# Projected pairs in an attention kernel: where the two sums of rows are issued, and in which order the products follow each other

## The chip, the cores and the metric

One NeuronCore of a Trainium2 chip runs the whole program. The metric is the device time of one execution in microseconds (us). The kernel before took 934.48 us (median of 3 runs, 934.42 to 935.12).

## The reference

Inputs are `x` of 16 batches x 100 rows x 640, and a context of 16 x 722 x 384 whose last 4 rows are "tokens". All is float32. Cut to what matters:

```python
enc, ca = ctx[:, :718], ctx[:, 718:]
hs      = mha(x @ Wq, enc @ Wk, enc @ Wv)           # 8 heads of 80, softmax over 718 keys
ca_q1   = einsum('btc,th->bch', ca, Wq_ca)[:, indices]
ca_hs1  = mha(ca_q1, x, x)
ca_hs2  = mha(ca_hs1 @ Wq, ca @ Wk_ca, ca @ Wv_ca)  # softmax over the 4 tokens
out     = (hs + ca_hs2) @ Wout + b_out + x
```

The change concerns the last line, the projection of the 1600 rows of `hs + ca_hs2` by the 640 x 640 matrix `Wout`, and the place of the weighted sum over the four tokens' values (in `ca_hs2`) on GpSimd's queue.

## The kernel before, in words

One loop runs over the 16 batches (L1198). The order of the work in it is written out by hand: the scheduler is told to keep it (L1197), so each engine takes its instructions in the order of the source. In a batch, TensorE makes the scores of three groups of keys (`scores`, L612), then, interleaved by hand, the blocks of this batch's values and of the next batch's keys (`vv.go`, `kk.go`, `both`; L432 and L463), then the last chunk of keys (`last_keys`, L557), the projection of earlier rows where enough rows are ready, the queries of the next two batches (L533, every second batch), and at the end the product of probabilities and values (L1417). Beside that VectorE takes maxima and subtracts them (L1232, L1220), ScalarE copies from PSUM and takes exponentials, and GpSimd does elementwise work on SBUF: scores of the tokens (L761, L768), the bias added to `x` (L895), probabilities of the tokens (L841), the weighted sum of the tokens' values (`values2`, L855 and L862), sums of context chunks (L498) and masked products (L709).

**The projection of a pair.** The 1600 rows are cut into chunks of 128, and ten of them are taken as five pairs. A pair is projected in the batch after the one that ended its rows, so in batches 3, 6, 8, 11 and 13 (`PAIRS`, L39). Of the 640 inner columns the first four chunks of 128 are multiplied by a scheme of seven block products in place of eight; the fifth chunk (`last(k)`) is added by plain products. The blocks are two chunks deep, so a block product is two matmuls of 128 x 128 by 128 x 320. Each float32 matmul is two records in the trace, hence 36 records for the 18 matmuls of a pair. `one` and `two` are the transposed rows of the pair's chunks, and `w(i, k)` the blocks of `Wout`.

The scheme needs sums of rows and of weights, all on GpSimd:

- `sums` (L986): `sum1` = the two blocks of `two` added, then the first block of `two` := `sum1` minus the first block of `one` (both L994). It is issued after `values2` (L1326 to L1328).
- in `project_pair` (L996): the second block of `one` is reduced by the first of `two` (L1030), the first block of `two` is replaced by the second minus itself (L1033), and the sum of weights `wout2[:, 0]` is reduced by `w(0, 0)` (L1034).

The products go into four PSUM banks, `b1`, `b2` of their own and `b3`, `b4`, the halves of one two-bank tile. `read(bank, j, k)` (L1022) has VectorE add a bank to the output rows of chunk `j`, columns half `k` (L1024, 128 x 320). `b1` is a running sum: it is read after each of its first three products and accumulated on, so each further product in `b1` waits until VectorE has read the bank. Between two uses of `b1` stand products in other banks.

The order before, in matmuls: `b1` 2, `b2` 3, `b1` 2 (needs the second L994), `b4` 3, `b1` 2 (with `sum1`), `b3` 2 (needs L1033 and L1034), `b1` 3 (needs L1030), `b3` 1.

**Queues.** SyncE issues most loads in order: in `values2` the third and fourth value rows `vb` (L810, each waits until GpSimd has used the buffer it goes into), then the next `xT` (some batches), `ca`, three pieces of `enc` (L218), `mb` (L700), two of `rest` (L231), and the output rows (L1048). GpSimd's own queue issues the first two `vb` of the next batch (L810) between `sums` and L1030.

Of the kernel before, what the change touches and what calls it, by code (L numbers as in the profile page):

```python
# [125 lines left out]
def kernel(  # L126
# [40 lines left out]
    def psumk(name):  # L167
        return psk.tile([P, 512], F32, tag="psk", name=name)
# [88 lines left out]
    wout2 = const.tile([P, 2, 2, H // 2], F32, name="wout2")  # L257
# [618 lines left out]
    class Last:  # L876
# [119 lines left out]
        def project_pair(self):  # L996

            r = PAIRS[self.b]
            one, two = hsTs[r], hsTs[r + 1]
            w = lambda i, k: wout_sb[  # L1000
                :, 2 * i : 2 * i + 2, k * (H // 2) : (k + 1) * (H // 2)
            ]
            last = lambda k: wout_sb[:, 4:, k * (H // 2) : (k + 1) * (H // 2)]
            both = pair(f"o_ps_{r}")
            b1, b2 = psumk(f"o_ps1_{r}"), psumk(f"o_ps2_{r}")
            b3, b4 = both[:, 0], both[:, 1]
            xn = self.xn
            less, more = ALU.subtract, ALU.add

            def product(to, terms, first):  # L1010
                steps = [(t[:, c], f[:, c]) for t, f in terms for c in range(t.shape[1])]
                for i, (t, f) in enumerate(steps):
                    nc.tensor.matmul(  # L1013
                        to[:, : H // 2],
                        t,
                        f,
                        start=first and i == 0,
                        stop=i == len(steps) - 1,
                        skip_group_check=True,
                    )  # L1020

            def read(bank, j, k):  # L1022
                part = xn[r + j][:, k * (H // 2) : (k + 1) * (H // 2)]
                nc.vector.tensor_tensor(part, bank[:, : H // 2], part, ALU.add)  # L1024

            product(b1, [(one[:, :2], w(0, 0))], True)
            read(b1, 0, 0)
            product(b2, [(one[:, 2:4], w(1, 0)), (one[:, 4:], last(0))], True)
            read(b2, 0, 0)
            nc.gpsimd.tensor_tensor(one[:, 2:4], one[:, 2:4], two[:, :2], less)  # L1030
            product(b1, [(two[:, :2], wout2[:, 0])], False)
            read(b1, 1, 0)
            nc.gpsimd.tensor_tensor(two[:, :2], two[:, 2:4], two[:, :2], less)  # L1033
            nc.gpsimd.tensor_tensor(wout2[:, 0], wout2[:, 0], w(0, 0), less)  # L1034
            product(b4, [(two[:, 2:4], wout2[:, 1]), (two[:, 4:], last(0))], True)
            read(b4, 1, 0)
            product(b1, [(sum1, w(0, 1))], False)
            read(b1, 1, 1)
            product(b3, [(two[:, :2], wout2[:, 0])], True)
            read(b3, 1, 0)  # L1040
            product(b1, [(one[:, 2:4], w(1, 1)), (one[:, 4:], last(1))], False)
            read(b1, 0, 1)
            product(b3, [(two[:, 4:], last(1))], False)
            read(b3, 1, 1)
            rows = out.rearrange("b s n -> (b s) n")
            for j in range(2):
                lo, n = OC[r + j]
                nc.sync.dma_start(out=rows[lo : lo + n], in_=xn[r + j])  # L1048
            xn.clear()
# [139 lines left out]
    last, enc_next, second_next = None, load_rest(1, load_enc(1)), Second(1, xT)  # L1189
# [8 lines left out]
    for b in range(B):  # L1198
        p = b // 2
        e_in, now = enc, second  # L1200
# [57 lines left out]
        if b == 0:  # L1258
            second.scores1()
            m_next = load_m(b + 2)  # L1260
            kk.go(3)
            top.go(3)
            first_values(3, e_in, (act, act), get=bank)
            top.go(1)
            kk.go(2)
            now.scores2()
            now.exponentials2()
            first_values(0, e_in, (act, act), (0,), bank)
            top.go()
            kk.go(3)  # L1270
            first_values(0, e_in, (act, act), (1,), bank)
            now.softmax3()
            kk.go(2)
            subtract(0)
            exponential(0)
            kk.go(2)
            subtract(1)
            kk.go(3)
            exponential(1)
            second_next, enc_next = loads()  # L1280
            less = subtract(2)
            exponential(2)
            last_keys(b + 1, enc)
            enc_next = load_rest(b + 2, enc_next)
            keys(m_next)
            now.values2(less)
            enc_sums(enc_next)
            second.softmax1(4)
        elif b + 1 < B:
            vv = Values(b, e_in)  # L1290

            def both(n):
                vv.go(n)
                kk.go(n)

            forms = [wout_sb[:, 2 * i : 2 * i + 2, k * (H // 2) : (k + 1) * (H // 2)]
                     for i in range(2) for k in range(2)]
            if b == 2:
                for o, left, right in (
                    (forms[1], forms[1], forms[0]),  # L1300
                    (wout2[:, 0], forms[3], forms[1]),
                    (wout2[:, 1], forms[2], wout2[:, 0]),
                ):
                    nc.gpsimd.tensor_tensor(o, left, right, ALU.subtract)
            elif last.b - 1 in PAIRS:
                nc.gpsimd.tensor_tensor(wout2[:, 0], wout2[:, 0], forms[0], ALU.add)
            second.scores1(seen, range(T - 1))
            top.go(3)
            both(3)
            now.scores2(nc.gpsimd)  # L1310
            second.scores1(None, range(T - 1, T))
            if b == 1:
                now.load()
            last.load()
            top.go(1)
            if b > 1:
                last.place()
            now.exponentials2()
            both(2)
            both(2)  # L1320
            top.go()
            both(1)
            now.softmax3()
            if b == 1:
                nc.gpsimd.tensor_tensor(last.hs[:S], last.hs[:S], last.hs2, ALU.add)
            now.values2()  # L1326
            if last.b in PAIRS:
                last.sums()  # L1328
            vv.go(2)
            kk.go(1)  # L1330
            subtract(0)
            exponential(0)
            vv.go(1)
            subtract(1)
            vv.go(1)
            kk.go(2)
            exponential(1)
            vv.go(1)
            kk.go(2)
            both(1)  # L1340
            both(1)
            if b == 1:
                for f in list(wv_there):
                    nc.scalar.copy(wv_sb[:, W_AT[f]], wv_there.pop(f))
            second.load()
            if b == 1:
                nc.gpsimd.dma_start(out=bias, in_=bout[0].partition_broadcast(P))
            second_next, enc_next = loads()
            if b + 2 < B:
                m_next = load_m(b + 2)  # L1350
            subtract(2)
            exponential(2)
            last_keys(b + 1, enc)
            if b + 2 < B:
                enc_next = load_rest(b + 2, enc_next)
            if b == 1:
                last.transpose()
            if last.b in PAIRS:
                second.softmax1(3)
                last.project_pair()  # L1360
                if last.b == max(PAIRS):
                    nc.sync.dma_start(
                        out=forms[1],
                        in_=wout[: 2 * P, H // 2 :].rearrange("(c p) n -> p c n", p=P),
                    )
            second.softmax1()
        else:
            room = enc_tile("spare").rearrange("p f k -> p (f k)")
            spare.extend(room[:, i * H : (i + 1) * H] for i in range(2))
            last.transpose()  # L1370
            vv = Values(b, e_in)
            last.load()
            mine.load()
            top.go(3)
            vv.go(3)
            last.project_few(len(OC) - 2)
            now.scores2(nc.gpsimd)
            now.exponentials2()
            top.go(1)
            vv.go(2)  # L1380
            top.go()
            vv.go(3)
            now.softmax3()
            now.values2()
            vv.go(2)
            subtract(0)
            exponential(0)
            vv.go(5)
            for i in (1, 2):
                subtract(i)  # L1390
                exponential(i)
            last.project()
# [49 lines left out]
        last = mine  # L1442
# [55 lines left out]
```

## Time and profile before

| what | us or share |
|---|---|
| median of 3 runs | 934.48 (934.42 to 935.12) |
| the profiled execution's own time | 933.03 |
| its span, first to last instruction | 931.3 |
| TensorE busy (matmul records) | 924.1, 99% |
| VectorE, ScalarE, GpSimd busy | 690.6 (74%), 433.8 (47%), 680.8 (73%) |
| granted TensorE clock | 0.999 |
| matmuls of the pairs (L1013) | 180 records of 0.432 us each, five stages |
| read of a bank (L1024) | 40 of 0.49 us |
| sums of rows (L994), in each pair | 0.72 and 0.73 or 0.74 us |
| L1030, L1033, L1034, in each pair | 0.74, 0.72, 1.53 us |
| one product and one sum of `values2` (L855, L862), undisturbed | 1.27 and 1.54 us |

The times of single instructions come from the timeline (start, length, engine, line, what is written from what, and in brackets how long the engine was idle before and who released it). PE rows are matmuls, PEld rows their weight loads, DVE is VectorE, ACT ScalarE, POOL GpSimd, and SP SyncE. Matmuls are pipelined: a record is 0.432 us long, and in an undisturbed run the next starts 0.269 us after it. So a stall is read from the distance of starts, not from the idle time in brackets.

### The profile page before, as it was taken

How to read it: one execution, taken by the hardware profiler on the slowest of the kernel's cores; microseconds unless marked ns; L12 is line 12 of the kernel's file. 1: busy time of each engine (PE TensorE's matmuls, PEld its weight loads, DVE VectorE, ACT ScalarE, POOL GpSimd, SP SyncE). 2: the span in 40 equal slices, each digit the busy share in tenths (PEclk: the TensorE clock that was granted, in tenths of full speed). 3: DMA queues.
4: the chain of work that ended last, by engine and by line, in shares of the span. 5: the costliest groups of instructions: out<-in, count | busy, mean ns of one | idle time of the engine just before them, and what ended most of it. 6: DMA issues, size and time to landing. Idle time of an engine off the chain costs nothing.

```text
span 931.3 us, 25889 instructions
## 1 busy us (share of the span) xinstructions
PE 924.1 (99%) x11130; PEld 786.7 (84%) x11130; DVE 690.6 (74%) x1080; ACT 433.8 (47%) x836; POOL 680.8 (73%) x646
## 2 busy tenths in 40 slices
PE   9999999999999999999999999999999999999998
PEld 6998989797797979888798788988879888798966
DVE  3859894989639896795967869579873898738884
ACT  2234543737336363652726436264641737417341
POOL 5757999788937878496874968658895588946723
PEclk9999999999999999999999999999999999999999
DMA  8822022040300304031030400204030050310201
GB/s 260 269 80 77 25 65 77 11 145 2 104 30 20 108 12 121 2 103 53 27 105 3 123 33 30 75 2 154 2 103 30 2 153 2 103 44 2 81 18 42
DMA packets 49673, 62.82 MB, mean 67 GB/s; under 512 B 14072, under 2 KB 38200, under 8 KB 49560
## 3 DMA queue, kind: packets, MB, share of 16 engines
q1 hardware_dynamic: 45512, 51.49, 18.0%
q0 software_dynamic: 3024, 8.53, 3.1%
q8 instruction: 87, 1.43, 0.6%
q10 hardware_dynamic: 1024, 1.15, 0.4%
q14 instruction: 26, 0.21, 0.1%
HBM read 55.59 MB, written 5.57 MB: 66 GB/s over the span
## 4 chain that ended last, share of the span: by engine, by line
PE 89%; POOL 7%; DVE 1%; DMA 1%; issue 1%; ACT 0%; POOLq 0%; DVEq 0%
PE s_ps L612 12%; PE a_ps L1417 12%; PE v_psA L432 9%; PE v_psB L432 8%; PE q_ps L533 7%; PE kT_ps L557 7%; PE k_psA L463 7%; PE k_psB L463 6%; PE o_ps L1013 4%; PE v_psC L432 3%; PE k_psC L463 2%; PE y_ps L736 2%; PE v_psD L432 2%; PE v_ps L373 2%; PE v_psE L432 2%; POOL e L761 1%
## 5 line engine op out<-in xcount | busy, mean ns | idle before, releaser
L761 POOL TENSOR_TENSOR e<-ca,g 100x800 f32<-100x800 f32 x64 | 99.5, 1564 | 127.0 <-DVE most L1232 113.1
L498 POOL TENSOR_TENSOR enc<-enc 128x240 f32<-128x240 f32 x135 | 105.9, 793 | 19.6 <-DMA enc<-in_enct 12.6
L1220 DVE TENSOR_TENSOR st<-st,over 120x1600 f32<-120x1600 f32 x48 | 115.5, 2407 | 0.0
L1417 PEld LDWEIGHTS a_ps<-vs,st 120*36 120x36 f32 (+3 forms) x3072 | 109.3, 125 | 5.3 <-issue 5.2
L1417 PE MATMUL a_ps<-vs,st 120*36 120x81 f32 (+3 forms) x3072 | 112.3, 233 | 0.2 <-issue 0.2
L432 PE MATMUL v_psA<-wv_sb,enc 128*120 128x320 f32 x352 | 109.8, 434 | 0.0
L862 POOL TENSOR_TENSOR hs<-hs,hs 100x640 f32<-100x640 f32 x48 | 103.7, 2160 | 3.8
L855 POOL TENSOR_TENSOR hs<-vb,p 100x640 f32<-100x640 f32 x64 | 91.7, 1444 | 8.9 <-issue 4.7
L612 PE MATMUL s_ps<-qp,kT 32*120 32x100 f32 x3072 | 97.8, 263 | 0.0
L612 PEld LDWEIGHTS s_ps<-qp,kT 32*120 32x120 f32 x3072 | 95.0, 179 | 1.7 <-issue 0.2
L629 ACT COPY st<-s_ps 120x800 f32<-120x800 f32 x64 | 49.7, 829 | 98.7 <-PE s_ps L612 98.7
L768 POOL TENSOR_TENSOR e<-e,e 100x800 f32<-100x800 f32 x48 | 92.2, 1920 | 3.8
L432 PE MATMUL v_psB<-wv_sb,enc 128*120 128x320 f32 x296 | 91.8, 433 | 0.0
L1228 ACT ACTIVATE st<-st 120x1600 f32<-120x1600 f32 x48 | 73.9, 1539 | 31.1 <-DVE st L1220 31.0
L463 PE MATMUL k_psA<-enc,wk_sb 128*128 128x240 f32 x360 | 87.7, 366 | 0.0
L1232 DVE TENSOR_TENSOR most<-most,st 120x800 f32<-120x800 f32 x64 | 68.2, 1065 | 22.4 <-ACT st L623 21.3
L463 PEld LDWEIGHTS k_psA<-enc,wk_sb 128*128 128x128 f32 x360 | 68.2, 190 | 16.8 <-DVE kT L403 0.2
L432 PEld LDWEIGHTS v_psA<-wv_sb,enc 128*120 128x120 f32 x352 | 63.2, 183 | 22.6 <-DVE vs L403 0.5
L463 PE MATMUL k_psB<-enc,wk_sb 128*128 128x240 f32 x300 | 73.1, 366 | 0.3 <-DVE sm L838 0.3
L432 PEld LDWEIGHTS v_psB<-wv_sb,enc 128*120 128x120 f32 x296 | 54.1, 183 | 21.9 <-DVE vs L403 0.4
L928 ACT COPY hsT<-turned_hs 32x160 f32<-32x160 f32 (+7 forms) x244 | 67.7, 278 | 3.0
L533 PE MATMUL q_ps<-xT,wq_sb 128*128 128x200 f32 x400 | 69.1, 333 | 0.0
(168 smaller groups left out, 1800.1 us busy)
## 6 DMA issues: line engine op xcount, KB each, us to landing
vb<-va_d POOLq DMA_DIRECT2D x32, 250.0 KB, 3.6
vb<-va_d SPq DMA_DIRECT2D x32, 250.0 KB
enc<-in_enct SPq DMA_DIRECT2D x30, 240.0 KB
enc<-in_enct SPq DMA_DIRECT2D x15, 360.0 KB
xT<-in_xt SPq DMA_DIRECT2D x8, 500.0 KB
rest<-in_enct SPq DMA_DIRECT2D x31, 120.0 KB
xn<-in_x SPq DMA_DIRECT2D x11, 320.0 KB
out<-xn SPq DMA_DIRECT2D x11, 320.0 KB
```

The costliest lines, as they stand in the source:

```text
L432: nc.tensor.matmul(at[0][j][:KN, : H // 2], a_form(self.enc, f)[:, j * KN : (j + 1) * KN], wv_there.get(f, wv_sb[:, W_AT[f]]), start=first ...
L463: nc.tensor.matmul(at[:, i * KT : (i + 1) * KT], wk_sb[:, W_AT[f], i], a_form(self.enc, f), start=(first and i == 0), stop=last, skip_grou ...
L498: nc.gpsimd.tensor_tensor(out, left, right, op)
L533: nc.tensor.matmul(q_ps[:, : 2 * S].rearrange("p (j s) -> p j s", j=2), wq_sb[:, c, n * P : (n + 1) * P], xT[:, :, c, :], start=(c == 0), ...
L612: nc.tensor.matmul(s_ps[r][:n, 256 * a + lo : 256 * a + hi], kT[rows, c, u, j * KN : (j + 1) * KN], rhs, start=(a == 0 and c == 0), stop=( ...
L761: first = nc.gpsimd.tensor_tensor(to, self.ca[:, t, :].unsqueeze(1).to_broadcast([S, NH, S]), g[:, :, t].unsqueeze(2).to_broadcast([S, NH, ...
L768: nc.gpsimd.tensor_tensor(e, e, to, ALU.add)
L855: first = nc.gpsimd.tensor_tensor(to, self.vb[t][:S].rearrange("p (h d) -> p h d", h=NH), p2[:, :, t].unsqueeze(2).to_broadcast([S, NH, D] ...
L862: nc.gpsimd.tensor_tensor(sums, sums, to, ALU.add)
L1220: return nc.vector.tensor_tensor(st[i], st[i], top.over[:KN].unsqueeze(1).to_broadcast([KN, 2, ROWS]), ALU.subtract,)
L1228: nc.scalar.activation(st[i], st[i], AF.Exp, scale=SCALE)
L1417: nc.tensor.matmul(a_v[lo:hi, h % 4], st[i // 2][: KEYS[i], i % 2, h * S + lo : h * S + hi], block(i, h // 4)[: KEYS[i], h % 4], start=(i ...
```

## The change

Two edits. In `project_pair` the order of the products is altered, the product of the fifth chunk with the second half of the columns moves from `b3` to a second use of `b2` (with a read of its own), and the product that needs the reduced sum of weights comes last and is then read twice. In the loop, `sums` is issued ahead of `values2`.

```diff
             product(b1, [(two[:, :2], wout2[:, 0])], False)
             read(b1, 1, 0)
             nc.gpsimd.tensor_tensor(two[:, :2], two[:, 2:4], two[:, :2], less)
             nc.gpsimd.tensor_tensor(wout2[:, 0], wout2[:, 0], w(0, 0), less)
-            product(b4, [(two[:, 2:4], wout2[:, 1]), (two[:, 4:], last(0))], True)
-            read(b4, 1, 0)
+            product(b4, [(two[:, 2:4], wout2[:, 1])], True)
             product(b1, [(sum1, w(0, 1))], False)
             read(b1, 1, 1)
+            product(b4, [(two[:, 4:], last(0))], False)
+            read(b4, 1, 0)
+            product(b2, [(two[:, 4:], last(1))], True)
+            read(b2, 1, 1)
+            product(b1, [(one[:, 2:4], w(1, 1)), (one[:, 4:], last(1))], False)
+            read(b1, 0, 1)
             product(b3, [(two[:, :2], wout2[:, 0])], True)
             read(b3, 1, 0)
-            product(b1, [(one[:, 2:4], w(1, 1)), (one[:, 4:], last(1))], False)
-            read(b1, 0, 1)
-            product(b3, [(two[:, 4:], last(1))], False)
             read(b3, 1, 1)
...
             now.softmax3()
...
-            now.values2()
             if last.b in PAIRS:
                 last.sums()
+            now.values2()
```

The order after, in matmuls: `b1` 2, `b2` 3, `b1` 2, `b4` 2, `b1` 2 (with `sum1`), `b4` 1, `b2` 1, `b1` 3, `b3` 2. It is 18 matmuls as before, nine reads in place of eight, and the same five operations on GpSimd, of which the two L994 stand ahead of the seven operations of `values2`.

## The prediction

> **What bounds the kernel now.** First the page's busy line and its chain of the work that ended last:
>
> ```profile
> PE 924.1 (99%) x11130; PEld 786.7 (84%) x11130; DVE 690.6 (74%) x1080; ACT 433.8 (47%) x836; POOL 680.8 (73%) x646
> PE 89%; POOL 7%; DVE 1%; DMA 1%; issue 1%; ACT 0%; POOLq 0%; DVEq 0%
> ```
>
> TensorE sets the time: the chain is 89% its own work, and only where another engine holds it up can a reordering gain. POOL's 7% is the one other part worth a look. The view of the line of the pairs' matmuls (L1013) says who holds them up:
>
> ```profile
> its engine sat idle before it (us, times) until:
>   POOL wout L1034: 2.6, 5
>   POOL hsT L994: 2.2, 4
> ```
>
> All by POOL: the second sum of rows (L994), which the second product in b1 needs, and the reduced sum of weights (L1034), which the product in b3 needs. These are idle times of the loads and matmuls added up; what TensorE lost is read from starts. The matmuls of the first pair (batch 3), then POOL beside them:
>
> ```profile
> 244.36 2.85 PE L1013 MATMUL o_ps<-wout_sb,hsT 128*128 128x320 f32 x10
> 247.59 2.42 PE L1013 MATMUL o_ps<-wout,hsT 128*128 128x320 f32 x8 [0.37 <-POOL hsT L994]
> 249.85 0.70 PE L1013 MATMUL o_ps<-wout_sb,hsT 128*128 128x320 f32 x2
> 250.38 1.24 PE L1013 MATMUL o_ps<-wout_sb,sum 128*128 128x320 f32 x4
> 251.68 1.34 PE L1013 MATMUL o_ps<-wout,hsT 128*128 128x320 f32 x4
> 252.86 2.32 PE L1013 MATMUL o_ps<-wout_sb,hsT 128*128 128x320 f32 x8
> 255.01 3.21 PE L533 MATMUL q_ps<-xT,wq_sb 128*128 128x200 f32 x18
> ```
>
> ```profile
> 244.50 1.54 POOL L862 TENSOR_TENSOR hs<-hs,hs 100x640 f32<-100x640 f32 x1
> 246.00 0.72 POOL L994 TENSOR_TENSOR sum<-hsT 128x256 f32<-128x256 f32 x1
> 246.80 0.74 POOL L994 TENSOR_TENSOR hsT<-sum,hsT 128x256 f32<-128x256 f32 x1
> 247.48 1.10 POOL L810 DMA_DIRECT2D vb<-va_d  x2
> 248.59 0.74 POOL L1030 TENSOR_TENSOR hsT<-hsT,hsT 128x256 f32<-128x256 f32 x1
> 249.40 0.72 POOL L1033 TENSOR_TENSOR hsT<-hsT 128x256 f32<-128x256 f32 x1
> 250.09 1.53 POOL L1034 TENSOR_TENSOR wout<-wout,wout_sb 128x640 f32<-128x640 f32 x1
> ```
>
> The last eight records run freely: 2.15 us, 0.269 each. Ten take 2.69, so the row at 247.59 should have begun at 247.05; L994 ended at 247.54. POOL goes from the last step of values2 (L862) through all seven rows almost without a gap: it is simply behind.
>
> **What can be gained.** A free stage of 36 records is 9.68. The five stages, from the first record to the first of the next work, last 10.65, 10.00, 9.99, 10.41 and 10.05 (pairs at 244, 415, 529, 691 and 807): 2.70 over it in all. By the place of the loss:
>
> - Before the second b1 product, and in its row (the second record starts 0.1 late after a stall): 0.54 + 0.11 at 244, 0 at 415 and 529, 0.30 + 0.11 at 691, 0.01 + 0.03 at 807. Sum 1.10.
> - Before b3 and in its row, each from the starts of sum's row, b3's row and the next, less 1.08 for four records: 0.32, 0.21, 0.20, 0.30, 0.32. Sum 1.35.
> - The other 0.2 lies at the step from the last record to L1417 after the pairs at 415 and 529 (0.1 each) and stays.
>
> **Part 1, sums ahead of values2.** It adds no work. POOL has its operands there: the wait of L841 for ScalarE, just ahead, covers the copies that fill the rows (the last ended at 226.4; the sums would start at 234.3). So the second sum is there over 10 us before TensorE asks, and the 1.10 goes. What is late next at that place is VectorE's first read of b1: at 244 it ends at 246.19, and the load it would release is due at 246.78. Values2 ends 1.5 later, where the sums ended before, so L810, L1030, L1033 and L1034 keep their times. Values2's result is added by VectorE only after the product with the probabilities, some 20 us on. SyncE's vb loads wait for values2, and ca (or xT and ca) stand behind them: 1.5 later each, with 1.0 to 1.5 us from the end of that later queue to enc's own release by TensorE (at 244: ca ended at 237.55, plus 1.5 is 239.05; enc was issued at 240.10). So the loads cost nothing; without that cover enc would come some tenths later, and its first reader, L498, stands behind L1034.
>
> **Part 2, the order of the products.** 18 matmuls before and after. b3 moves from the 25th record to the 33rd. Its load is due at start + 31 x 0.269: 252.70 at 244, against L1034's end of 251.62 plus 0.05 for the release (at 415: end 422.16, load at 422.21). Slack 1.03; at the others 1.77, 1.77, 1.27 and 1.62. So the 1.35 goes too. b1's last product needs L1030, which ended 1.7 us before its load would be due.
>
> The price: b1's further products have two matmuls (four records, 1.08 us) as cover where the sum had three. No row shows a four-record cover without a stall by POOL in it, so I bound it. VectorE at the pair at 415, behind its own work:
>
> ```profile
> 416.56 0.64 DVE L676 TENSOR_REDUCE mx<-side 32x25 f32<-32x100 f32 x2
> 417.23 0.49 DVE L1024 TENSOR_TENSOR xn<-o_ps,xn 128x320 f32<-128x320 f32 x1
> 418.53 0.49 DVE L1024 TENSOR_TENSOR xn<-o_ps,xn 128x320 f32<-128x320 f32 x1 [0.82 <-PE o_ps L1013]
> 419.67 0.49 DVE L1024 TENSOR_TENSOR xn<-o_ps,xn 128x320 f32<-128x320 f32 x1 [0.64 <-PE o_ps L1013]
> ```
>
> The last one is the read that sum1's product waits for. Its matmul's last record started at 419.14 and the read ended 1.02 later; with 0.05 for the release that is 1.07, and the load is due after 1.08. Even a late load costs little: at 807 the load that waited for L994 stood idle 0.27 and TensorE lost 0.04; at 691 idle 0.64 lost 0.41. About 0.23 is free. So I take 0. The upper end: 0.2 at each of ten such places, 2.0. The lower end is 0, since a wait gives nothing back.
>
> The ninth read is 0.49 of VectorE in each pair, and now two reads follow the last product where one did; the last ends some 0.3 later than now. Behind it stand L694 and L778 (ends at 428.5 at the pair at 415), for an exponential that TensorE needs after L1417 and the next scores, 14 us on. Hidden; without the cover 0.5 a pair. The first use of b2's bank by the queries is now behind that bank's second read, which ends some 1.8 us before it is wanted.
>
> **One rule against the change.** The same subtraction on VectorE (L1220, 48 times) takes 1.77 to 3.10 us, and POOL's L855 takes 1.27 alone and 2.74 beside one that starts at 410.88. The Trainium skill, SBUF — State Buffer, section "Who interferes with whom", says that a VectorE operation with two SBUF inputs and a GpSimd operation that reads SBUF shut each other out, and the first to start keeps the port. By that rule other POOL operations would meet the subtractions, and values2 would end at another time than 1.5 later; one hold more by it would make the sum 1.75.
>
> By the rows each of a pair's three subtractions costs POOL about 1.5, whatever it meets, since POOL has work throughout. One hold more (1.5 against a slack of 1.03 or 1.27) would leave 0.5 and 0.2 of stall at 244 and 691; the others absorb it. I keep the 2.45 and this 0.7 for the range.
>
> **Sum.** 1.10 + 1.35 = 2.45. The profiled execution's 933.03 would become 930.58. The median of the runs is 1.45 above that execution, with nothing to say where; I take the same 2.45 off: 934.48 - 2.45 = 932.0. A change under 0.2% (1.9 us) is about what measurement can't tell from none.
>
> **The rivals.**
>
> - *The reads set the pace* (the cover of two matmuls falls short at ten places). For: slack of 0.01 by the rows. Against: 0.23 free. At 0.1 a place, 1.0 is given back: 933.0.
> - *POOL's end slips* by a hold: 0.7 given back, 932.7. For: the subtractions shift against POOL's queue. Against: the same three holds in every pair.
> - *The time is waited for elsewhere*: TensorE comes to L1417 earlier and waits for the exponentials: 934.5. Against: the third subtraction ended at 413.8 and its exponential takes 1.54, with L1417 due at 425.6.
> - *Slower: VectorE comes late to the first read of b1.* At 415, 529 and 807 that read follows L676 at once, so it moves with the third subtraction, which may have to wait for a POOL operation. Up to 0.5 it is free (0.29 of slack at 415 and the 0.23), and late by x it costs about 3 times x - 0.5, so from x = 1.3 it eats the gain. Late by 2.0, it costs 4.5 there, and at 244 and 691, where the read now starts 0.7 and 0.9 after L676 and is done 0.5 before the load, 0.6 and 0.3: 937.4. Against: the subtraction there took 2.95 already, and none of 48 took over 3.10.
>
> **How the numbers follow.** Forecast 0.60, the reads 0.18, POOL 0.09, elsewhere 0.08, slower 0.05. Range: up to 934.0 (the reads' upper end, 2.0 given back, is 934.0); down to 931.0, should the runs that are 1.45 longer than the profiled one have lost part of it, say 1.0, at these same waits. It leaves out the last two cases. Faster by over 0.2% (below 932.6): the forecast and part of the POOL case, 0.63. Slower: 0.05. Within: 0.32.
>
> **What would show it.** Right: L1013 idle for POOL near 0; five stages of 9.7 to 9.8; L994 some 10 us ahead of the stage, L1034 at the same distance from the stage's start, and b3's row without idle time. The reads: rows with sum or the last b1 product start over 1.08 after the fourth record before, released by DVE L1024. POOL: L1034 ends over 8.3 after the stage's start. Elsewhere: L1417 or L533 waiting. What makes me wrong: a wait of the new order I priced at 0.

## The result, and the profile after

The changed kernel took 930.79 us (median of 6 runs, 929.97 to 931.6) where the kernel before took 934.68 in the same measurement (6 runs, 934.1 to 935.12): ratio 0.9959, 95% interval 0.9946 to 0.9972. That is 3.9 us faster by the medians (2.6 to 5.0 by the interval) where 2.45 was forecast, and 0.2 us below the range. The profiled execution took 931.33, span 929.5.

The page's busy line and its chain, as shown of before:

```profile
PE 922.4 (99%) x11130; PEld 787.6 (85%) x11130; DVE 693.2 (75%) x1085; ACT 433.9 (47%) x836; POOL 678.2 (73%) x646
PE 97%; DVE 2%; DMA 0%; issue 0%; ACT 0%; POOL 0%; ACTq 0%; DVEq 0%
```

POOL's 7% of the chain is gone, and VectorE has the five reads more. In the view of line L1013 the list of what its engine waited for is empty: there is no row between its heading and "who waited for it". The matmuls of the first pair, then POOL:

```profile
244.40 2.86 PE L1013 MATMUL o_ps<-wout_sb,hsT 128*128 128x320 f32 x10
247.09 2.32 PE L1013 MATMUL o_ps<-wout,hsT 128*128 128x320 f32 x8
249.25 1.24 PE L1013 MATMUL o_ps<-wout_sb,sum 128*128 128x320 f32 x4
250.32 2.85 PE L1013 MATMUL o_ps<-wout_sb,hsT 128*128 128x320 f32 x10
253.02 1.24 PE L1013 MATMUL o_ps<-wout,hsT 128*128 128x320 f32 x4
254.09 2.19 PE L533 MATMUL q_ps<-xT,wq_sb 128*128 128x200 f32 x12
```

```profile
231.16 1.82 POOL L841 TENSOR_TENSOR p<-e,sm 100x32 f32<-100x32 f32 x1
232.95 0.73 POOL L994 TENSOR_TENSOR sum<-hsT 128x256 f32<-128x256 f32 x1
233.75 2.25 POOL L994 TENSOR_TENSOR hsT<-sum,hsT 128x256 f32<-128x256 f32 x1
...
245.96 1.54 POOL L862 TENSOR_TENSOR hs<-hs,hs 100x640 f32<-100x640 f32 x1
247.44 1.10 POOL L810 DMA_DIRECT2D vb<-va_d  x2
248.55 0.74 POOL L1030 TENSOR_TENSOR hsT<-hsT,hsT 128x256 f32<-128x256 f32 x1
249.36 0.73 POOL L1033 TENSOR_TENSOR hsT<-hsT 128x256 f32<-128x256 f32 x1
250.05 1.54 POOL L1034 TENSOR_TENSOR wout<-wout,wout_sb 128x640 f32<-128x640 f32 x1
```

VectorE's reads of the pair at 415, which stood behind its own work in the kernel before too:

```profile
414.86 0.66 DVE L676 TENSOR_REDUCE mx<-side 32x25 f32<-32x100 f32 x2
416.40 0.49 DVE L1024 TENSOR_TENSOR xn<-o_ps,xn 128x320 f32<-128x320 f32 x1 [0.89 <-POOL hs L855]
...
421.19 1.57 DVE L1024 TENSOR_TENSOR xn<-o_ps,xn 128x320 f32<-128x320 f32 x3 [1.60 <-PE o_ps L1013]
423.88 0.49 DVE L1024 TENSOR_TENSOR xn<-o_ps,xn 128x320 f32<-128x320 f32 x1 [1.12 <-PE o_ps L1013]
424.96 0.89 DVE L1024 TENSOR_TENSOR xn<-o_ps,xn 128x320 f32<-128x320 f32 x2 [0.59 <-PE o_ps L1013]
```

VectorE is now early: it sits idle ahead of the first read, where in the kernel before it went straight from L676 to that read. Three later reads come in a row, and the last two follow the last product; all the later ones are released by TensorE. (The view names POOL for the first, but it starts 0.52 after the start of its product's last record, as reads that TensorE released do.) TensorE waits for none of them: in the matmuls of the first pair, every start is the one before plus 0.269 a record. The five stages last 9.69, 9.78, 9.78, 9.69 and 9.69: 48.64 in all where the first profile of before has 51.09. The second L994 ends over 8 us ahead of each stage, some 11 ahead of the product that needs it. L1034 ends 7.18 after the first stage's start where it ended 7.26 after it. So each step of the mechanism stands as forecast, and against the first profile the stages lost exactly the 2.45. What does not fit is the total: by the runs it is 3.9, by these two profiled executions 933.03 - 931.33 = 1.7.

### The profile page after: what moved, and what is told of

Same layout as the page of the kernel before. It is cut to its first block, busy times and chain, and to the rows that moved or that the text cites. A ratio compares the mean times of both kernels' runs of the same rounds, so it can differ in the third digit from the quotient of the medians.

```text
span 929.5 us, 25894 instructions
## 1 busy us (share of the span) xinstructions
PE 922.4 (99%) x11130; PEld 787.6 (85%) x11130; DVE 693.2 (75%) x1085; ACT 433.9 (47%) x836; POOL 678.2 (73%) x646
## 4 chain that ended last, share of the span: by engine, by line
PE 97%; DVE 2%; DMA 0%; issue 0%; ACT 0%; POOL 0%; ACTq 0%; DVEq 0%
PE s_ps L612 12%; PE a_ps L1419 12%; PE v_psA L432 11%; PE v_psB L432 9%; PE kT_ps L557 8%; PE k_psA L463 7%; PE q_ps L533 7%; PE k_psB L463 6%; PE o_ps L1013 5%; PE v_psC L432 3%; PE k_psC L463 3%; PE v_psD L432 2%; PE v_psE L432 2%; PE y_ps L736 2%; PE v_ps L373 1%; PE k_psE L463 1%
## 5 line engine op out<-in xcount | busy, mean ns | idle before, releaser
L761 POOL TENSOR_TENSOR e<-ca,g 100x800 f32<-100x800 f32 x64 | 99.4, 1564 | 126.8 <-DVE most L1234 99.7
L498 POOL TENSOR_TENSOR enc<-enc 128x240 f32<-128x240 f32 x135 | 106.7, 800 | 19.7 <-DMA enc<-in_enct 12.7
L432 PE MATMUL v_psA<-wv_sb,enc 128*120 128x320 f32 x352 | 109.8, 434 | 0.0
L862 POOL TENSOR_TENSOR hs<-hs,hs 100x640 f32<-100x640 f32 x48 | 100.5, 2095 | 3.8
L855 POOL TENSOR_TENSOR hs<-vb,p 100x640 f32<-100x640 f32 x64 | 89.6, 1411 | 9.5 <-issue 4.7
L432 PE MATMUL v_psB<-wv_sb,enc 128*120 128x320 f32 x296 | 91.8, 433 | 0.0
L432 PEld LDWEIGHTS v_psA<-wv_sb,enc 128*120 128x120 f32 x352 | 63.2, 183 | 22.6 <-DVE vs L403 0.5
L432 PEld LDWEIGHTS v_psB<-wv_sb,enc 128*120 128x120 f32 x296 | 54.1, 183 | 21.9 <-DVE vs L403 0.4
```

Source lines behind the costliest of these rows:

```text
L432: nc.tensor.matmul(at[0][j][:KN, : H // 2], a_form(self.enc, f)[:, j * KN : (j + 1) * KN], wv_there.get(f, wv_sb[:, W_AT[f]]), start=first ...
L498: nc.gpsimd.tensor_tensor(out, left, right, op)
L761: first = nc.gpsimd.tensor_tensor(to, self.ca[:, t, :].unsqueeze(1).to_broadcast([S, NH, S]), g[:, :, t].unsqueeze(2).to_broadcast([S, NH, ...
L855: first = nc.gpsimd.tensor_tensor(to, self.vb[t][:S].rearrange("p (h d) -> p h d", h=NH), p2[:, :, t].unsqueeze(2).to_broadcast([S, NH, D] ...
L862: nc.gpsimd.tensor_tensor(sums, sums, to, ALU.add)
```

## The theories

- *A*: the waits for POOL cost more in a usual execution of before than in the one the forecast was worked from; the change takes all of them.
- *B*: the waits are the same in every execution. The profiled one was short for other reasons, and the change gains something the stages do not show.

The table has every profiled execution. "Stages" are the five stretches from the first record of a pair to the first of the next work; the two losses are read from the starts around the second product in b1 (L994) and the product in b3 (L1034); "rest" is time less stages.

| execution | time | stages | lost at L994 | lost at L1034 | rest |
|---|---|---|---|---|---|
| before, the one shown | 933.03 | 51.09 | 1.07 | 1.38 | 881.94 |
| before, second | 934.79 | 52.08 | 2.08 | 1.37 | 882.71 |
| before, third | 934.31 | 52.00 | 1.98 | 1.39 | 882.31 |
| after | 931.33 | 48.64 | 0 | 0 | 882.69 |
| after, second | 930.37 | 48.64 | 0 | 0 | 881.73 |
| sums ahead alone | 934.04 | 51.76 | 0 | 3.12 | 882.28 |
| order alone | 934.76 | 51.51 | 2.88 | 0 | 883.25 |
| order alone, second | 935.11 | 51.80 | 3.16 | 0 | 883.31 |
| order alone, third | 933.92 | 50.80 | 2.17 | 0 | 883.12 |
| before, one POOL operation more | 937.62 | 54.78 | 1.98 | 4.17 | 882.84 |
| after, one POOL operation more | 930.86 | 48.64 | 0 | 0 | 882.22 |
| after, cover of one matmul | 933.85 | 50.51 | 0 | 1.88 (reads) | 883.34 |
| before without the pairs' bias | 931.16 | 48.64 | 0 | 0 | 882.52 |
| after, b3 read between | 936.64 | 54.76 | 0 | 1.88 + 4.25 (reads) | 881.88 |
| before, POOL's start let go | 931.44 | 49.43 | 0.13 | 0.66 | 882.01 |

In the two rows with "(reads)" the loss is VectorE's reads at other places.

## The experiments

**The kernel before, twice more** (no edit).

> The kernel before, unchanged, for a second profiled execution: the one the forecast was made from took 933.03, the runs 934.1 to 935.12. Theory A (what the profiled execution showed too little of is the very waits for POOL in the five pairs; POOL came later in the runs): the five stages exceed 9.68 by some 4 us in all, not 2.70, in an execution of about 934.5, and L994 and L1034 end later against the stage's start. Theory B (the waits in the pairs are the same in every execution, the 1.45 us lies in other places, such as issue stalls or the loads at the start): the stages exceed 9.68 by 2.5 to 2.9 again and the extra time is found elsewhere along the chain.

> A third profiled execution of the kernel before, to tell a property of the kernel from chance. Theory A: again some 4 us over 9.68 in the five stages. Theory B: 2.5 to 2.9 again, the rest elsewhere and at places that differ between the executions.

934.79 and 934.31. Of the second execution, the view of line L1013, and the matmuls of the pair in batch 11:

```profile
  POOL hsT L994: 4.1, 6
  POOL wout L1034: 2.6, 5
```

```profile
693.21 2.85 PE L1013 MATMUL o_ps<-wout_sb,hsT 128*128 128x320 f32 x10
696.79 2.42 PE L1013 MATMUL o_ps<-wout,hsT 128*128 128x320 f32 x8 [0.73 <-POOL hsT L994]
```

The idle time for L1034 is the 2.6 of the first profile; that for L994 is 4.1 in place of 2.2. The second row starts 3.58 after the first where 2.69 is free: 0.90 lost, with 0.10 more in the row, against 0.40 in the first profile. The stages exceed five times 9.68 by 3.7 and 3.6. That is A in kind, a little under its 4; B's 2.5 to 2.9 is excluded.

**Each part alone.** The edits are the two halves of the diff: `sums` ahead of `values2` with the old order of products, and the new order with `sums` behind.

> Part 1 alone: the sums of rows ahead of values2, the products in the old order. It leaves the wait for L1034. By the prediction's terms the wait for L994 (1.10) goes: 933.6 against 934.7. Theory A, with 3.9 gained in all shared like the 2.45: about 1.7 gained, 932.9. Theory B, where the terms are right and the rest is gained by something else: 1.1 and a part of 1.4 more that the stages do not show. In the profile: no idle time for L994, the row with b3 still late by 0.2 to 0.5 or more, since POOL is as late as before and TensorE comes earlier.

> Part 2 alone: the new order of products, the sums behind values2. It leaves the wait for L994. By the prediction's terms the wait for L1034 (1.35) goes: 933.3 against 934.7. Theory A: about 2.1 gained, 932.6. Theory B: 1.35 and a part of 1.4 more that the stages do not show. In the profile: the wait for L994 as before at the pairs of batches 3 and 11, none at b3.

Sums ahead alone: 933.81 (ratio 0.9991, 0.9983 to 1.0). Order alone: 932.55 (ratio 0.9985, 0.9976 to 0.9994); seven of its twelve runs lie at 931.8 to 932.8, the others at 933.1 to 935.7. The sums fall short of the 932.9 that I expected by A and are hardly clear of no gain. The order has the expected 932.6 as its median, but by the ratio, which goes by the means, it gained 1.4 in place of 2.1. The first pair with the sums ahead says why they gain so little:

```profile
247.02 2.32 PE L1013 MATMUL o_ps<-wout,hsT 128*128 128x320 f32 x8
...
249.71 1.24 PE L1013 MATMUL o_ps<-wout_sb,sum 128*128 128x320 f32 x4
251.47 1.34 PE L1013 MATMUL o_ps<-wout,hsT 128*128 128x320 f32 x4 [0.51 <-POOL wout L1034]
```

The row for L994 is on time. The b3 row comes 1.76 after sum's where 1.08 is free: 0.68, and 0.10 in the row. TensorE arrives earlier, POOL does not, and the wait for L1034 takes over: 3.12 in all in place of 1.4. The two waits stand in series behind one late engine. The wait at L994 costs nothing more once the one at L1034 follows, so moving the sums gains little by itself. The new order alone takes the wait at L1034 away in each execution and leaves the one at L994. So my 1.10 for the sums was not what that part is worth alone; only both together move what TensorE needs from POOL out of the way.

**Order alone, twice more**, for its two groups of runs (no further edit).

> Part 2 alone once more, since its runs fell into two groups, near 932.2 and near 934.7, and the profiled one was of the upper group with 2.9 us lost at L994. If the groups differ by how late POOL comes, an execution of the lower group shows 0.5 or less lost there; if by something else, 2.9 again.

> Part 2 alone for a third execution, with the same two outcomes to tell apart: 0.5 or less lost at L994 in an execution near 932.2, or 2.9 again whatever the time.

935.11 with 3.16 lost at L994, 933.92 with 2.17. Time and loss go together over the three executions; none fell into the lower group, so what that group lost was not seen.

The loss at L994 is larger here than in the three executions of before (1.07, 2.08, 1.98), but the new order did not bring it about inside the stage: it is larger in the first pair already, ahead of which nothing of the new order has run (0.87, 1.06 and 1.10, in before 0.64, 0.41 and 0.45). There POOL's chain of the batch (L761) started 28.33 to 28.41 ahead of the stage, in before 28.74 to 28.84. A late start goes with a large loss, as the last experiment takes up; why it was late in all three is open.

**One POOL operation more**, the same edit on before and on the changed kernel, ahead of the first product:

```diff
+            scratch = product_tile(f"scratch_{r}")[:, : 4 * P // 2].rearrange("p (c s) -> p c s", c=2)
+            nc.gpsimd.tensor_tensor(scratch, two[:, 2:4], two[:, 2:4], more)
```

> The kernel before with one more operation of about 0.72 us on POOL at the start of each projection, ahead of L1030, onto a scratch tile that nothing reads. If POOL is what TensorE waits for in every pair (theory A), each of the five waits for L1034 grows by 0.7 to 0.8: 3.5 to 4.0 slower than before, 938.3. If the end is set by something else and POOL's waits take up slack (theory B): less than 2.

> The changed kernel with the same operation at the same place. By the slack that the new order leaves at the product in b3 (1.0 to 1.8 us by the prediction, and 0.2 that a late load has free): no change, 930.8. If the slack is not there, up to 4 slower than the changed kernel, 934.8.

Before: 937.29 (ratio 1.0031, 1.0019 to 1.0043), 2.7 slower. The operation took 0.62 and set the rest back by 0.57, less than the 0.72 I took. The five waits for L1034 grew by 0.55 or so each, in all from 1.38 to 4.17: POOL's delay is passed on whole. On the changed kernel: 931.09 (0.9963, 0.9949 to 0.9977), no loss. POOL of its first pair, whose b3 row began at 252.77:

```profile
247.98 0.63 POOL L1027 TENSOR_TENSOR scratch<-hsT 128x256 f32<-128x256 f32 x1
...
250.04 1.54 POOL L1036 TENSOR_TENSOR wout<-wout,wout_sb 128x640 f32<-128x640 f32 x1
```

The sum of weights ends at 251.58, 1.2 before the row starts, and 0.9 before its load is due. The slack is real.

**POOL's lateness taken away without the change.** In the kernel before, the bias added to the ten paired chunks (L895) is left out, 3.1 us of POOL's work ahead of the sums in each pair; order and place of the sums stay, and the output of those chunks lacks the bias.

```diff
-                    nc.gpsimd.tensor_tensor(to, to, bias[at : at + n, cols], ALU.add)
+                    if n <= 64 or r >= 10:
+                        nc.gpsimd.tensor_tensor(to, to, bias[at : at + n, cols], ALU.add)
```

> The kernel before, order and all, without the bias that POOL adds to the rows of the pairs (L895, two operations of 1.54 us or more in each pair's batch; the output of the ten paired chunks lacks the bias). POOL then comes to the sums 3.1 us earlier in each pair's batch. Theory A (the whole gain of the change is POOL's lateness at the two waits, 3.4 us in a usual execution): as fast as the changed kernel, 930.8 to 931.3, five stages of 9.7 to 9.8. If the order of the products has a worth of its own: 1 us or more slower than the changed kernel, with stalls for VectorE's reads in the stages.

930.82 (ratio 0.9961, 0.9949 to 0.9974), beside 930.96 (0.9961, 0.9949 to 0.9974) of the changed kernel in a further measurement:

> The changed kernel, unchanged, for a tighter interval and a second profiled execution. Theory A (the waits for POOL in the pairs cost 3.4 us in a usual execution of before, by its two further profiles, and the change takes all of them): 3.4 to 3.9 faster than before, stages of 9.69 and 9.78 with no idle time for POOL. Theory B (a part of the 3.9 comes from elsewhere): the same total, but the stages differ by less than 3.0 from those of before.

The stages are 48.64 in both. The second sum ends 1.0 to 1.3 after the stage's start, 1.1 to 2.6 earlier than in the three executions of before. With POOL in time, the old order runs as freely as the new one: the order has no worth beyond the time it gives POOL, and POOL's lateness was the whole of the loss in the stages. But the old order has no reserve. POOL of the first pair (line numbers one higher than in before):

```profile
248.53 0.73 POOL L1034 TENSOR_TENSOR hsT<-hsT 128x256 f32<-128x256 f32 x1 [0.88 <-PE o_ps L1014]
249.21 1.54 POOL L1035 TENSOR_TENSOR wout<-wout,wout_sb 128x640 f32<-128x640 f32 x1
```

Now POOL waits for TensorE: the first operation overwrites rows that the second product in b1 reads. In this order the sum of weights can't come earlier, and the load of b3's product came 0.16 late in all five pairs. That cost 0.005 at most, but any more would show.

**What the reads cost**, the price I had bounded. Cover is what stands in other banks between a product and the next use of its bank. First, one matmul of cover in place of two ahead of b1's last product:

```diff
-            product(b2, [(two[:, 4:], last(1))], True)
-            read(b2, 1, 1)
             product(b1, [(one[:, 2:4], w(1, 1)), (one[:, 4:], last(1))], False)
             read(b1, 0, 1)
+            product(b2, [(two[:, 4:], last(1))], True)
+            read(b2, 1, 1)
```

> The changed kernel with the second product in b2 moved behind the last one in b1, so that only one matmul (two records, 0.54 us) stands between the product with sum1 and the last product in b1. By the working of the prediction, the read and its release take 1.02 to 1.07 from the start of the last record, the load is due after 0.54, and 0.23 is free: 0.25 to 0.3 at each pair, 1.3 to 1.5 in all, 932.2. If a wait for a read costs the whole 1.0 or more each time, 5 us: 935.8. If reads cost nothing at this cover either, 930.8.

932.94 (ratio 0.9987, 0.9978 to 0.9996), 2.0 more than the changed kernel; each pair lost 0.38. Then no cover at all: the second use of b2 is taken back, and the fifth chunk's product stays in b3, behind the first read of it.

```diff
-            product(b2, [(two[:, 4:], last(1))], True)
-            read(b2, 1, 1)
...
             product(b3, [(two[:, :2], wout2[:, 0])], True)
             read(b3, 1, 0)
+            product(b3, [(two[:, 4:], last(1))], False)
             read(b3, 1, 1)
```

> The changed kernel without the second use of b2: the fifth chunk's product with the second half of the columns stays in b3, behind the read of the product with the sum of weights. Now one matmul stands before the last product in b1 (0.38 a pair, by the run with that cover) and none before the last product in b3: read and release 1.07 from the start of the last record where the next load is due at once, 0.16 free: about 0.9. Together 1.3 a pair, 6.4 in all: 937.3. If reads cost less than I think without cover, 933 to 935.

936.81 (ratio 1.0022, 1.0011 to 1.0034), slower than before. In its first pair:

```profile
249.96 2.69 PE L1013 MATMUL o_ps<-wout_sb,hsT 128*128 128x320 f32 x8
252.49 1.24 PE L1013 MATMUL o_ps<-wout,hsT 128*128 128x320 f32 x4
254.31 0.81 PE L1013 MATMUL o_ps<-wout_sb,hsT 128*128 128x320 f32 x2 [0.58 <-DVE xn L1024]
```

The last row starts 1.82 after the one before where 1.08 is free: 0.75, and 0.10 in the row, 0.85 a pair. The first row, of eight records, has 2.53 to the next in place of 2.15: the 0.38 of the cover of one. So two matmuls of cover cost 0, one 0.38, none 0.85 in each pair. The second use of b2, which looks like a by-product of the reordering, is what the new order can't do without.

**POOL's start let go.** In the executions of before, the loss at L994 goes with the start of POOL's chain in that batch: with L761 29.06 before the stage 0.03 was lost, with 28.74 0.64, with 28.42 1.14. The program holds that start until VectorE's last maximum (L1232). The run takes this ordering away; the data waits stay.

```diff
-            second.scores1(seen, range(T - 1))
+            second.scores1(None, range(T - 1))
```

> The kernel before without the ordering that holds POOL's first score product (L761) until VectorE's last maximum (L1232); its data waits stay. In the executions of before, POOL's lateness at L994 goes with the start of that product, 28.4 to 29.1 us ahead of the stage. If that start is what sets the wait, POOL now starts up to 2 us earlier (its inputs are there then), less what the maxima hold it up, 0.5 to 1.5 net: the wait for L994 falls from 2.0 to 0.7 or less and that for L1034 shrinks too, stages 49 to 50.5 in place of 52.0. If POOL's lateness comes from further on in its chain, the stages stay near 52. The time may be worse elsewhere, as the maxima then meet POOL's products.

931.55 (ratio 0.9966, 0.9951 to 0.9981). The third execution of before, and below it this run, in the batch of the pair at 692 and 691:

```profile
663.95 3.04 POOL L761 TENSOR_TENSOR e<-ca,g 100x800 f32<-100x800 f32 x2 [3.67 <-PE v_psD L432]
```

```profile
660.79 4.41 POOL L761 TENSOR_TENSOR e<-ca,g 100x800 f32<-100x800 f32 x2 [1.66 <-issue]
```

In the first row the view names a matmul (L432) as the releaser, but the product starts 0.24 after the end of the last maximum (663.71), and without the ordering it starts earlier. The products then start 30.55 ahead of the stage in place of 28.42 and take 1.4 longer; POOL comes 1.1 earlier to the sums, and the stages fall to 49.43. So the start sets the wait, and one word in the kernel before gives most of the change's gain. What moves the start by 0.7 from execution to execution is only argued: VectorE's maxima ahead of it took 2.43 for two in the first profile and 2.88 in the third, beside POOL's L498, and no run took these apart.

## Why the prediction was wrong

- *Sums ahead: the wait at L994 goes.* Right. *The size, 1.10*: this is the term that failed. It was read from one execution and taken for the usual one; that execution lost 1.07 there, two others 2.08 and 1.98.
- *The new order: the wait at L1034 goes, 1.35.* Right in mechanism and size: 1.37 to 1.39 in all three executions. In the pairs with a stall at L994 this wait repeats because the stall has just brought TensorE into step with POOL, and the wait at L994 takes up whatever lateness POOL comes with. In the pairs at 415 and 529, where nothing is lost at L994, POOL itself repeats: L1034 ended 6.48 to 6.53 after the stage's start.
- *L1030 to L1034 keep their times; slack of 1.03 and more at b3.* Right as far as it matters: over the five pairs L1034 ended 6.6 to 7.2 after the stage's start, in the first profile of before 6.5 to 7.3, so 1.07 or more was left; and 0.57 of added work cost nothing.
- *VectorE's reads with two matmuls of cover cost 0.* Right, but the free part of a late load is smaller than I read: with one matmul of cover the load came 0.54 late and cost 0.38, with none 1.01 late and cost 0.85, so 0.16 is free, not 0.23. The idle times of loads from which I took 0.23 hold 0.08 (0.269 less the load's own 0.190) that every load in a free stream has ahead of it.
- *The port on SBUF.* The second L994 took 2.25 beside a subtraction that started at 233.60, where it took 0.74 alone. The rule of the Trainium skill, SBUF — State Buffer, section "Who interferes with whom", that the first to start keeps the shared port, fits this row. It cost nothing in the end, since POOL still ended ahead of TensorE's need in every pair.
- *The same 2.45 off the median.* This is where the mis-sized term entered. The runs of before were 1.45 above the profiled execution, and I wrote that nothing says where. By the table about 0.95 of it lay in the stages (52.04, the mean of the two further executions, against 51.09), at the wait for L994; outside the stages these two were 0.4 and 0.8 longer than the first, which is scatter. The lower end of the range gave 1.0 for more loss at these waits and nothing for scatter, so it ended at 931.0. The sign of being wrong that the prediction named, a wait of the new order priced at 0, did not appear.

The forecast with 2.0 for 1.10 would have been 934.5 - 3.4 = 931.1. That lies well within the interval of 2.6 to 5.0. The last 0.2 to 0.5 of the measured 3.6 to 3.9 is not assigned: outside the stages the executions of all kernels lie between 881.7 and 883.3, those of before at 882.3 and those of after at 882.2 in the mean, so no gain is shown there. This scatter has fixed places. Of the six stretches ahead of, between and behind the stages, three last the same to 0.02 in all 15 executions; the others are the one ahead of the first stage (244.0 to 245.0), the one behind it (160.6 to 162.0) and the one behind the fourth (104.3 to 105.4). The largest single gaps in the last two lie in the product with the values (L1417), near 317 and near 765: up to 1.0 at one of them or at both, and the profile names nothing that TensorE waits for there. The executions of order alone and of the cover of one matmul, with the largest rests (883.1 to 883.3), have a gap at both. What makes these gaps is open.

## What to carry to other kernels

Where a late engine feeds one chain at two places, price the places together: the first wait hides part of the second, and removing the first alone moved the loss to the second here. A stall's size in one profiled execution is one draw; when the runs lie above that execution, look first at the waits whose releaser has a moving start. Here they held about 0.95 of the 1.45. A bank that is read and accumulated on needs cover for the whole way round by the reading engine, here two matmuls, and a second use of a free bank can be what buys that cover.

## What the runs showed of the hardware

- A load of weights came 0.16 us late at no cost (POOL's bias left out). Beyond that, the matmul's two records together lost the lateness less 0.16: 0.19 late cost 0.03 (the first profile, pair at 807), 0.54 cost 0.38, 1.01 cost 0.85. Up to 0.105 of that loss shows only at the second record.
- From the start of a product's last record to the end of VectorE's read of 128 x 320, where TensorE released it, took 0.96 to 1.03 us, and a load that waited for the read started 1.01 (no cover) or 1.08 (one matmul) after that start. Four records 0.269 apart, 1.08, cover it.
- Time outside the stages was the same to 0.8 us either way over 15 executions of 10 different kernels, and all of the scatter lay in three of six stretches.
